# An adaptive-weight FFN in split fp32r on one core: moving the last pairs' gate, evictions and column steps

## The chip, the cores and the metric

The kernel runs on one core of a Trainium2 chip. The time is device microseconds of one execution; the median of three runs of the kernel before is 414.88 us (414.72 to 414.88). Engines are named as in the profile: PE (TensorE, matrix products), DVE (VectorE), ACT (ScalarE), POOL (GpSimd), SP (SyncE, which only queues DMAs here).

## The reference

The input x has 64 batches of 64 rows and 1024 columns. Each batch picks one of 16 matrices of 64 x 64, and its 64 rows are mixed by it. The mixed rows go through a 1024 x 1024 layer, and a small low-rank branch is added for the one of four experts that wins a linear gate. The result is added to x.

```python
W = weights[condition]                      # one 64 x 64 matrix per batch
m = einsum('bct,bcd->bdt', x, W)            # mix the 64 rows of each batch
logits = m @ gate_w.T + expert_bias         # 4 experts
top1 = argmax(logits)
base = einsum('bth,oh->bto', m, W_up)       # 1024 -> 1024
z = einsum('nh,erh->ner', m, lora_A)        # 4 experts x rank 8
d = einsum('ner,ehr->neh', z, lora_B)       # SCALE is 1
out = x + base + d[top1]
```

## The kernel before

**Order of the algebra.** Mixing rows and multiplying by weights commute, so the kernel multiplies x first, by a matrix of 1060 columns: 4 columns of the gate, 32 of lora_A and 1024 of W_up. That product is called u. It then applies the row mix to u (the block diagonal matrix `bd` holds two batches' matrices), takes gate and low-rank values from the first 36 columns, and adds the low-rank branch.

**Tiles.** 128 rows (two batches) are one block; there are 32 blocks, worked on in 16 pairs (a, b). A column half has 530 columns (NB), and a product over half of the 1024 inner elements has four k steps. To keep fp32's accuracy every factor is split in a high and a low part, and three matmuls (high x high, low x high, high x low) make one step; each is cut in two PSUM banks of 264 and 266 columns. A k step is thus six matmuls.

**Pairs and products.** The first two pairs use eight half products each (`eight`). The others use a scheme with seven (`seven`), for which the activations and the weights are summed first (S1 to S4, T1 to T4). `order` in `seven` lists the products. The last pair has six in its list; the seventh (S4 by B22) is done after the list by `product_by_bank`, one bank after the other, so that the first bank can be read while the second is computed. `c` is the name of the accumulators of products (three of 1024 columns), `o` that of smaller ones (two of 512 columns).

**Column steps.** A block's output is made in column steps, for most blocks of 356, 352 and 352 columns (`COLS`), for the last but one block (a of the last pair) of 356, 174, 258 and 272 (`LAST`). One column step is `apply` (three matmuls with `bd`), `delta` (one matmul adding the low-rank branch) and `evict`; `finish` is all three. The first step is split, since the gate needs its first 36 columns: `apply`, then `gate` (six small DVE operations that pick the expert and mask the low-rank values, to z), then `turn` (a transpose of z on PE, its two parts copied by ACT and DVE to zt), then `delta` and `evict`.

**Evictions.** For all blocks but the last two, `evict` copies `o` by ACT to a y tile; three y tiles exist. After the last column step POOL queues a DMA that adds x to the tile in place, and SP queues the store when it has landed. The last pair's two y tiles are loaded ahead with x: b's are added by DVE and stored by ACT's queue, column step by column step; a's first 494 columns go by ACT and an accumulating DMA (480 of them are then stored, 14 go with the next store), the rest by DVE and SP's queue. So in the last pair the block ahead (pb, block 29) has to use the y tile of the block before it (pa, block 28).

**What sets the order.** All instructions are kept in program order on their engine (`InOrder`, line 35). The program order is written by hand: `at(s, k, fn, ...)` puts a step into product s after k step k, and k = -1 ahead of the product. In the last pair, up to the change, step 3 is S3 by T3, step 4 is A22 by T4 (accumulator "4", b's first half), and step 5 is S1 by T1. pb's first step is evicted at (3, 2), its others finish at (3, 3) and (4, 1). The gate of a is at (4, 2), its `turn` at (5, 1) and its `delta` at (5, 2). `first_of_b` at (5, -1) makes the first 36 columns of b's u; `gate_of_b` at (5, 1) takes the gate from them in the first bank of an accumulator of its own, `ts["w"]`. A `c` buffer, `z`, receives the transpose of b's z in its first bank and b's first column step in its second.

In the profile nearly all lines are line 43, that of the helper which keeps program order, so tile names are what tells instructions apart: `uh`/`ul` are u's parts, `ah`/`al` those of activations, `bd` the row mix, `lg` to `z` the gate, `o<-ident,z` the transpose.

Of the kernel before, what the change touches and what calls it, by code (L numbers as in the profile page):

```python
# [46 lines left out]
def kernel(  # L47
# [28 lines left out]
    tensor, vector, scalar, pool, sync = (  # L76
        InOrder(tc, e) for e in (nc.tensor, nc.vector, nc.scalar, nc.gpsimd, nc.sync)
    )
# [17 lines left out]
    raw, As, us, ys, wsel, zs, os_, ts = ({} for _ in range(8))  # L96

    def temp(name):
        return tp.tile([P, NB], F32, name=name, tag="t")
# [95 lines left out]
    def chain():  # L195
        return psum.tile([P, 1024], F32, name="c", tag="c", bufs=3)
# [38 lines left out]
    def body(c):  # L235
        return c[:, LEFT : LEFT + NB]
# [7 lines left out]
    def u_low(i, n, src):  # L244
        h, lo = us[i]
        vector.tensor_sub(lo[:, n], src, h[:, n].bitcast(F32))

    def u_split(i, n, src):
        scalar.copy(u_tiles(i)[0][:, n], src)
        u_low(i, n, src)  # L250

    def half(hf):
        return slice(NB * hf, NB * hf + NB)

    def u_of(i, hf, c):
        u_split(i, half(hf), body(c))
# [5 lines left out]
    def u_sum(i, hf, c, t):  # L262
        u_add(i, c, t)
        u_split(i, half(hf), ts["u", i])
# [33 lines left out]
    STORED = FIRST // 16 * 16  # L298

    def place():  # L300
        return psum.tile([P, 512], F32, name="o", tag="o", bufs=2)
# [10 lines left out]
    def apply(i, j, o=None):  # L312
        c0, n = cols(i, j)
        o = os_[i, j] = place() if o is None else o
        cond_u(o[:, :n], i, slice(c0, c0 + n))
# [33 lines left out]
    def delta(i, j):  # L349
        s, d = ycols(i, j)  # L350
        tensor.matmul(
            os_[i, j][:, s], zs[i], b3[:, d], start=False, stop=True, skip_group_check=True
        )
# [22 lines left out]
    def finish(i, j, o=None):  # L376
        apply(i, j, o)
        delta(i, j)
        evict(i, j)
# [60 lines left out]
    u = raw[0, 0][:, k]  # L440
# [181 lines left out]
    def seven(g):  # L622
        a, b = 2 * g, 2 * g + 1
        last = g == NG - 1
        h = [[] for _ in range(7)]
        pa, pb = a - 2, a - 1
        cp = cs[g - 1]

        def at(s, k, fn, *args):
            h[s].append((k, fn, *args))  # L630

        def first_of_b():

            s = ts["last"] = temp("usum")
            q, r = slice(0, G), slice(G, NB)
            vector.tensor_add(s[:, q], body(c["4"])[:, q], ts["t7"][:, q])
            u_split(b, q, s[:, q])
            vector.tensor_add(s[:, r], body(c["4"])[:, r], ts["t7"][:, r])

        def gate_of_b():  # L640
            ts["w"] = chain()
            o = ts["w"][:, :512]
            cond_u(o[:, :G], b, slice(0, G))
            gate(b, o)
            u_split(b, slice(G, NB), ts["last"][:, G:])

        if g == 2:
            at(0, 0, apply, pa, 0)
            at(0, 0, gate, pa)
            at(0, 0, lambda: u_of(pb, 0, cp["1"]))  # L650
            at(0, 3, turn, pa)
            at(1, 0, delta, pa, 0)
            at(1, 0, evict, pa, 0)
            at(1, 1, finish, pa, 1)
            at(1, 2, finish, pa, 2)
            for k in range(KH):
                at(1 + k, 3, split_b, "T4", k)
            at(1, 3, apply, pb, 0)
            at(1, 3, gate, pb)
            at(2, 3, turn, pb)  # L660
        else:
            at(0, -1, lambda: u_sum(pb, 0, cp["2"], ts["t1"]))
            at(0, 1, finish, pa, 1)
            at(0, 3, finish, pa, 2)
            at(1, 2, apply, pb, 0)
            at(1, 2, gate, pb)
            at(2, 2, turn, pb)
        at(3, 2, delta, pb, 0)
        at(3, 2, evict, pb, 0)
        at(3, 3, finish, pb, 1)  # L670
        at(4, 1, finish, pb, 2)
        at(1, -1, lambda: keep("t1", c["1"]))
        if not last:
            order = (
                ("1", "A11", "B11", True),
                ("2", "S2", "T2", True),
                ("3", "S1", "T1", True),
                ("1", "A12", "B21", False),
                ("2", "S3", "T3", False),
                ("3", "S4", "B22", False),  # L680
                ("2", "A22", "T4", False),
            )
            at(0, 2, split_a, g, "S1")
            at(1, 0, split_a, g, "A12")
            at(2, 0, lambda: keep_sum("t6", c["2"], "t1"))
            at(2, 1, split_a, g, "S3")
            at(2, 2, split_cond, a)
            at(3, -1, lambda: keep_sum("t5", c["3"], "t1"))
            at(3, 2, split_a, g, "S4")
            at(4, -1, lambda: u_of(a, 0, c["1"]))  # L690
            at(4, 2, split_a, g, "A22")
            at(5, -1, lambda: u_add(b, c["2"], ts["t5"]))
            at(5, 0, apply, a, 0)
            at(5, 0, gate, a)
            at(5, 0, lambda: u_split(b, half(1), ts["u", b]))
            at(6, 0, turn, a)
            at(6, 0, lambda: u_sum(a, 1, c["3"], ts["t6"]))
            at(6, 2, delta, a, 0)
            at(6, 2, evict, a, 0)
            at(6, 3, split_cond, b)  # L700

            for i in (b + 2, a + 2):
                at(0, 0, load_half, i, 0)
                at(1, 0, load_half, i, 1)
            at(1, 3, load_cond, a + 2)
            at(3, 1, load_cond, b + 2)
            at(2, 3, sums, g + 1, "S1")
            at(3, 3, sums, g + 1, "S2")
            at(4, 3, sums, g + 1, "S3")
            at(5, 2, split_a, g + 1, "A11")  # L710
            at(6, 1, split_a, g + 1, "S2")
            at(6, 3, sums, g + 1, "S4")
            if g == NG - 2:
                for i in (a + 2, b + 2):
                    at(6, 0, load_y, i)
        else:

            order = (
                ("1", "A11", "B11", True),
                ("2", "S2", "T2", True),  # L720
                ("1", "A12", "B21", False),
                ("2", "S3", "T3", False),
                ("4", "A22", "T4", True),
                ("3", "S1", "T1", True),
            )
            at(0, 2, split_a, g, "A12")
            at(1, 0, split_a, g, "S3")
            at(2, 0, lambda: keep_sum("t6", c["2"], "t1"))
            at(2, 1, split_a, g, "A22")
            at(2, 2, split_cond, a)  # L730
            at(3, -1, lambda: u_of(a, 0, c["1"]))
            at(3, 0, split_a, g, "S1")
            at(3, 1, split_cond, b)
            at(4, -1, lambda: keep_sum("t7", c["2"], "t1"))
            at(4, 0, split_a, g, "S4")
            at(4, 2, apply, a, 0)
            at(4, 2, gate, a)
            at(5, -1, first_of_b)
            at(5, 1, turn, a)
            at(5, 1, gate_of_b)  # L740
            at(5, 2, delta, a, 0)
            at(5, 2, evict, a, 0)
            at(5, 3, lambda: finish(a, 1, ts["w"][:, 512:]))
        run(g, order, h, c)
        cs[g] = dict(c)
        if last:

            z = chain()
            turn(b, z[:, :512])
            u_add(b, c["3"], ts["t7"])  # L750
            scalar.copy(us[b][0][:, half(1)], ts["u", b])
            keep_sum("t8", c["3"], "t6")
            s = temp("usum")
            places = place(), place()

            def u_bank(m):
                n = LAST_BANKS[m]
                vector.tensor_add(s[:, n], places[m][:, : n.stop - n.start], ts["t8"][:, n])
                scalar.copy(us[a][0][:, NB + n.start : NB + n.stop], s[:, n])

            def u_bank_low(m):
                n = LAST_BANKS[m]
                u_low(a, slice(NB + n.start, NB + n.stop), s[:, n])

            product_by_bank(
                g,
                places,
                "S4",
                "B22",
                [(3, u_bank, 0), (3, lambda: u_low(b, half(1), ts["u", b]))],  # L770
            )
            u_bank(1)
            u_bank_low(0)
            finish(b, 0, z[:, 512:])
            u_bank_low(1)
            finish(b, 1, chain()[:, :512])
            sync.dma_start(out[a, :, :STORED], ys[a][:, :STORED])
            finish(b, 2, chain()[:, :512])
            finish(a, 2)
            finish(a, 3)  # L780
# [50 lines left out]
```

## Time and profile before

| What | us |
|---|---|
| median of three runs | 414.88 |
| the profiled execution | 415.4 |
| its span, first to last instruction | 413.6 |
| PE busy in the span | 408.5 |
| DVE, ACT, POOL busy | 285.6, 185.0, 75.0 |
| step 3 of the last pair starts on PE | 391.61 |
| last matmul starts / takes | 409.39 / 0.29 |

The table's first two rows are the time of an execution, the others are inside the span. A row of the timeline gives start, duration, engine, operation, tiles (out<-in), shape, and in brackets how long the engine sat idle before it and what ended that. Rows of the same shape that follow each other are merged (x2). Matmuls are pipelined: their durations overlap, so what one costs is the distance of two starts, 0.12 us for 264 columns. A row of the table by stretches gives the stretch, its length, busy time and number of instructions for PE, PEld (weight loads), DVE, ACT and POOL, then the granted clock of PE, the mean busy share of the 16 DMA engines and GB/s.

### The profile page before, as it was taken

How to read it: one execution, taken by the hardware profiler on the slowest of the kernel's cores; microseconds unless marked ns; L12 is line 12 of the kernel's file. 1: busy time of each engine (PE TensorE's matmuls, PEld its weight loads, DVE VectorE, ACT ScalarE, POOL GpSimd, SP SyncE). 2: the span in 40 equal slices, each digit the busy share in tenths (PEclk: the TensorE clock that was granted, in tenths of full speed). 3: DMA queues.
4: the chain of work that ended last, by engine and by line, in shares of the span. 5: the costliest groups of instructions: out<-in, count | busy, mean ns of one | idle time of the engine just before them, and what ended most of it. 6: DMA issues, size and time to landing. Idle time of an engine off the chain costs nothing.

```text
span 413.6 us, 8160 instructions
## 1 busy us (share of the span) xinstructions
PE 408.5 (99%) x3191; PEld 407.7 (99%) x3191; DVE 285.6 (69%) x648; ACT 185.0 (45%) x419; POOL 75.0 (18%) x92
## 2 busy tenths in 40 slices
PE   8999999999999999999999999999999999999996
PEld 8999999999999999999999999999999999999995
DVE  5987776876767666676676767666676676766766
ACT  5846734453534445333343534445333344533531
POOL 4304502020020202102020020202102020020000
PEclk9999999999999999999999999999999999999999
DMA  8889964553556435465453555434465443564345
GB/s 276 301 305 224 241 167 98 137 123 99 172 133 177 92 93 143 124 178 135 103 127 98 164 135 159 128 81 138 122 179 135 104 126 94 169 165 124 52 101 178
DMA packets 25830, 60.99 MB, mean 147 GB/s; under 512 B 3328, under 2 KB 5344, under 8 KB 25792
## 3 DMA queue, kind: packets, MB, share of 16 engines
q1 hardware_dynamic: 18112, 40.48, 27.2%
q0 software_dynamic: 6704, 19.21, 27.1%
q10 hardware_dynamic: 976, 0.79, 0.6%
q8 instruction: 25, 0.41, 0.4%
q14 instruction: 13, 0.11, 0.1%
HBM read 43.68 MB, written 16.78 MB: 146 GB/s over the span
## 4 chain that ended last, share of the span: by engine, by line
PE 97%; DMA 1%; issue 0%; POOL 0%; DVE 0%; POOLq 0%
PE c L43 81%; PE o L43 16%; DMA cond_sb<-in_cond_dram 1%; DVE y L43 0%; POOL which L43 0%; POOL condf L43 0%; POOLq L43 0%; POOLq L818 0%
## 5 line engine op out<-in xcount | busy, mean ns | idle before, releaser
L43 PE MATMUL c<-hT,ah 128*128 128x264 f32 x480 | 139.7, 291 | 0.0
L43 PE MATMUL c<-lT,ah 128*128 128x264 f32 x480 | 137.3, 286 | 0.0
L43 PE MATMUL c<-hT,al 128*128 128x264 f32 x480 | 137.1, 286 | 0.0
L43 PE MATMUL c<-hB,ah 128*128 128x264 f32 (+1 forms) x424 | 121.8, 289 | 0.0
L43 PE MATMUL c<-hB,al 128*128 128x264 f32 (+1 forms) x424 | 121.0, 287 | 0.0
L43 PE MATMUL c<-lB,ah 128*128 128x264 f32 (+1 forms) x424 | 119.0, 287 | 0.0
L43 PEld LDWEIGHTS c<-lT,ah 128*128 128x128 f32 x480 | 91.0, 190 | 0.0
L43 PEld LDWEIGHTS c<-hT,ah 128*128 128x128 f32 x480 | 90.9, 189 | 0.0
L43 PEld LDWEIGHTS c<-hT,al 128*128 128x128 f32 x480 | 90.6, 189 | 0.0
L43 POOL DMA_DIRECT2D y<-in_x_dram x31 | 29.3, 945 | 290.3 <-ACT y L43 285.3
L43 PEld LDWEIGHTS c<-hB,ah 128*128 128x128 f32 x424 | 80.7, 190 | 0.3 <-ACT hB L43 0.2
L43 PEld LDWEIGHTS c<-hB,al 128*128 128x128 f32 x424 | 80.7, 190 | 0.0
L43 PEld LDWEIGHTS c<-lB,ah 128*128 128x128 f32 x424 | 79.5, 190 | 0.2 <-issue 0.2
L43 ACT COPY y<-o 128x352 f32<-128x352 f32 (+1 forms) x91 | 40.1, 443 | 58.4 <-PE o L43 55.0
L43 ACT CAST uh<-usum 128x530 fp32r<-128x530 f32 (+4 forms) x44 | 27.1, 616 | 68.4 <-DVE usum L43 68.4
L43 DVE TENSOR_TENSOR al<-S,ah 128x512 fp32r<-128x512 f32 x56 | 38.5, 688 | 24.2 <-ACT ah L43 24.2
L43 DVE TENSOR_TENSOR al<-xh,ah 128x512 fp32r<-128x512 f32 x46 | 31.7, 689 | 30.0 <-ACT ah L43 30.0
L43 PE MATMUL o<-uh,bd 128*128 128x356 f32 (+2 forms) x186 | 44.7, 322 | 0.0
L43 DVE TENSOR_TENSOR ul<-usum,uh 128x530 fp32r<-128x530 f32 (+4 forms) x44 | 30.0, 682 | 18.6 <-ACT uh L43 18.6
L43 ACT CAST zt<-o 96x128 fp32r<-96x128 f32 x31 | 8.1, 262 | 76.0 <-PE o L43 76.0
L43 POOL DMA_INDIRECT wsel<-in_cw_dram,idx x32 | 34.9, 1089 | 10.6 <-issue 5.2
L43 ACT CAST ah<-S 128x512 fp32r<-128x512 f32 x56 | 34.9, 623 | 1.8 <-DVE S L43 1.4
(88 smaller groups left out, 471.3 us busy)
## 6 DMA issues: line engine op xcount, KB each, us to landing
xh<-in_xt_dram SPq DMA_DIRECT2D x60, 256.0 KB
y<-in_x_dram POOLq DMA_DIRECT2D x30, 512.0 KB, 5.6
out_dram<-y SPq DMA_DIRECT2D x30, 512.0 KB
wraw<-in_w_dram SPq DMA_DIRECT2D x23, 265.0 KB
T<-in_w_dram POOLq DMA_DIRECT2D x8, 265.0 KB, 7.3
xx<-in_xt_dram SPq DMA_DIRECT2D x1, 512.0 KB
wsel<-in_cw_dram,idx POOLq DMA_INDIRECT x32, 5.0
y<-in_x_dram SPq DMA_DIRECT2D x1, 512.0 KB
```

The lines of the kernel that those rows point to most:

```text
L43: return lambda *a, **k: self.tc.keep_in_program_order(fn(*a, **k))
```

## The change

Only what the last pair issues is changed. The block ahead's first step is evicted after k step 0 of step 3, and its others finish after (3, 1) and (4, 0). The gate of a moves to the end of step 3, its transpose to (4, 1), its `delta` and eviction to (5, 0), and its second column step to (5, 2), where it takes an `o` buffer in place of the second half of `ts["w"]`. The store of a's first 480 columns is queued in step 5, ahead of the last pair's other stores in SP's order. In the last product b's first column step is put between the two banks, and the low part of a's first bank after k step 1 of the second bank; the second bank's low part moves behind b's second column step.

```diff
-        at(3, 2, delta, pb, 0)
-        at(3, 2, evict, pb, 0)
-        at(3, 3, finish, pb, 1)
-        at(4, 1, finish, pb, 2)
+        for step, where in enumerate(((3, 0), (3, 1), (4, 0)) if last else ((3, 2), (3, 3), (4, 1))):
+            if step:
+                at(*where, finish, pb, step)
+            else:
+                at(*where, delta, pb, 0)
+                at(*where, evict, pb, 0)
...
-            at(4, 2, apply, a, 0)
-            at(4, 2, gate, a)
+            at(3, 3, apply, a, 0)
+            at(3, 3, gate, a)
+            at(4, 1, turn, a)
             at(5, -1, first_of_b)
-            at(5, 1, turn, a)
+            at(5, 0, delta, a, 0)
+            at(5, 0, evict, a, 0)
             at(5, 1, gate_of_b)
-            at(5, 2, delta, a, 0)
-            at(5, 2, evict, a, 0)
-            at(5, 3, lambda: finish(a, 1, ts["w"][:, 512:]))
+            at(5, 2, finish, a, 1)
+            at(5, 3, lambda: sync.dma_start(out[a, :, :STORED], ys[a][:, :STORED]))
...
-                [(3, u_bank, 0), (3, lambda: u_low(b, half(1), ts["u", b]))],
+                [
+                    (3, u_bank, 0),
+                    (3, lambda: u_low(b, half(1), ts["u", b])),
+                    (3, lambda: finish(b, 0, z[:, 512:])),
+                    (5, u_bank_low, 0),
+                ],
             )
             u_bank(1)
-            u_bank_low(0)
-            finish(b, 0, z[:, 512:])
+            finish(b, 1, chain()[:, :512])
             u_bank_low(1)
-            finish(b, 1, chain()[:, :512])
-            sync.dma_start(out[a, :, :STORED], ys[a][:, :STORED])
             finish(b, 2, chain()[:, :512])
             finish(a, 2)
             finish(a, 3)
```

## The prediction

> **What bounds the kernel now.** I read the page first: who is busy, and what chain ended last.
>
> ```profile
> PE 408.5 (99%) x3191; PEld 407.7 (99%) x3191; DVE 285.6 (69%) x648; ACT 185.0 (45%) x419; POOL 75.0 (18%) x92
> ...
> PE 97%; DMA 1%; issue 0%; POOL 0%; DVE 0%; POOLq 0%
> ```
>
> TensorE is busy 408.5 of 413.6 us. The change adds and removes no matmul and touches only what is issued after about 391.6 us. So there are two places where time can move: holes that appear in TensorE's row (today there are none there), and what follows its last matmul.
>
> Next the timeline of the last 20 us. First ScalarE (ACT) from step 3 of the last pair on, where the pair ahead is evicted:
>
> ```profile
> 391.86 0.60 ACT L43 CAST uh<-c 128x530 fp32r<-128x530 f32 x1
> 392.49 0.62 ACT L43 CAST ah<-S 128x512 fp32r<-128x512 f32 x1
> 393.02 0.51 ACT L43 CAST bd<-wsel 64x64 fp32r<-64x64 f32 x2
> 395.44 0.78 ACT L43 COPY y<-o 128x320 f32<-128x320 f32 x2 [1.91 <-DMA out_dram<-y]
> 396.24 0.62 ACT L43 CAST ah<-S 128x512 fp32r<-128x512 f32 x1
> ```
>
> The last row but one is the one to see. The eviction of pb's first columns (128x320) was computed by TensorE at 393.81+0.31 = 394.12, but ACT sat 1.91 us until 395.44: the y buffer that it writes still held the row block before, whose store (queued by SyncE at 392.71) had not landed. Nothing upstream of that store is moved by the change, so 395.44 stays. Today all urgent ACT work (uh, ah, bd) is ahead of this copy in ACT's queue, and nobody needs pb's buffer soon, so the wait is free.
>
> Then what the gate of a costs, and TensorE at the end:
>
> ```profile
> 398.92 0.16 DVE L43 TENSOR_TENSOR lg<-o,bias_sb 128x4 f32<-128x4 f32 x1 [1.33 <-PE o L43]
> ...
> 400.04 0.25 DVE L43 COPY z<-zm 128x96 f32<-128x96 f32 x1
> ...
> 400.94 0.27 PE L43 MATMUL o<-ident,z 128*96 128x128 f32 x1
> ...
> 409.39 0.29 PE L43 MATMUL o<-b,zt 96*128 96x272 f32 x1
> ```
>
> The gate takes 400.29-398.92 = 1.37 us on VectorE (DVE). The last matmul ends at 409.68, the last eviction at 410.16 (409.24+0.92), and the span at 413.6. What fills the 3.4 us after it, by stretches (the last two columns are DMA share and GB/s):
>
> ```profile
> 408.50:409.00 0.50, 0.50 (x6) 0.50 (x5) 0.50 (x2) 0.00 (x0) 0.00 (x0) 1.00 0.00 0
> 409.00:409.50 0.50, 0.50 (x6) 0.46 (x4) 0.50 (x2) 0.00 (x0) 0.00 (x0) 1.00 0.94 342
> ...
> 411.75:412.00 0.25, 0.00 (x0) 0.00 (x0) 0.00 (x0) 0.00 (x0) 0.00 (x0) 1.00 0.81 287
> 412.00:412.50 0.50, 0.00 (x0) 0.00 (x0) 0.00 (x0) 0.00 (x0) 0.00 (x0) 1.00 0.02 4
> ```
>
> Six stores are still to be moved at 409.0 (160, 240, 2 x 176 and 2 x 136 KB, 1.05 MB) and keep all 16 DMA engines full until about 412.05: 345 GB/s. The last store waits behind the others.
>
> **The change part by part.**
>
> *The tail (gain).* finish(b, 0) moves ahead of the second bank. Its four matmuls (0.49+0.33+0.31 as pitch: 0.64 us) only change places with the bank, so TensorE's end is unmoved; VectorE's y copy of 320 columns now comes right after ul of 530 columns, and its store leaves about 0.7 us earlier on its own clock. The 240 KB store of a leaves earlier too: its accumulating DMA was issued at 404.33 and the store at 408.30, 3.97 later; finish(a, 1) now ends one k step (0.73) sooner. So 400 KB leave the burst ahead of the rest. VectorE keeps up: y 320, ul 258, usum 272, y 352, ul 272 at pitches of 0.35 to 0.43 put ul 272 ready 0.25 us before its matmul (409.27); today it is 0.8 ahead. If that cover went, the cost would be that difference alone. What is left then is bounded by the last three stores, b's third (issued at about 409.4) and a's two (409.7, 410.19). The row gives 0.87 us from issue to data (first ACT issue 408.14, data from 409.0), so they start at 410.35, and 448 KB at 345 GB/s take 1.33: 411.7 instead of 412.05. Against this row stands the price of the Trainium skill ("DMA: Bandwidth & Descriptors", section on the anatomy of one DMA, SWDGE path; these stores are of the other kind): the variable part is bytes over 436 GB/s, which would give 1.05 us and 411.4, a gain of 0.65, but then the last store's own 410.19+0.87+0.4 = 411.47 is the limit, 0.58. I take the measured rate: **-0.38**, ends -0.2 and -0.58.
>
> *The pair ahead by two k steps.* delta and evict of pb go from (3, 2) to (3, 0), its two finishes from (3, 3) and (4, 1) to (3, 1) and (4, 0). TensorE's inputs are there: zt of pb is done at 391.66, and delta now comes at 392.34. But the copy of pb's first columns now stands in ACT's queue directly behind uh, ahead of ah (S1) and the two bd casts, and still starts at 395.44. The Trainium skill ("TensorE: Matmul & The Clock Gate", engine queue depths) says that the ACT and DVE queues are strictly first in, first out. This is the rule that speaks against the change, and the row of 1.91 us idle agrees as far as it can: nothing overtook. With it, everything behind the copy is held from 392.5 to 395.44. Were it not so, only the owner of the buffer would be late.
>
> *The gate of a, up a product (from (4, 2) to (3, 3), the transpose from (5, 1) to (4, 1)).* Two accumulators of 512 columns ("o") exist. In the new order pb's first columns hold one, and the second is free when the transpose of pb is read. finish(pb, 1) takes that one without a wait; the gate column of a has to take the one of pb's first columns, so its first matmul waits for ACT. Step 3 starts at 391.61, a k step takes 0.735, delta 0.15, a finish of 352 columns 0.65. The gate column is due at 391.61+0.735+0.15+0.735+0.65+1.47 = 395.35. The buffer is free at 395.44+0.43 = 395.87; with 0.13 for the wait and the weight load (390.65 to 390.77 at the transpose) it starts at 396.0. **Stall one: 0.65.**
>
> Second, z. ACT by the pitches of the rows: y 320 at 395.44, ah 395.76, y 352 at 396.28 (+0.53), bd 396.63 (+0.34), bd done 397.14. DVE's queue, in order: al of S1 from 396.41, bd from 397.01 to 397.5, and only then the gate: lg at 397.51, z done at 398.88, transpose at 399.06 (0.05 for the semaphore, 0.13 load). TensorE, already 0.65 late, comes there at 396.0+0.49+0.735+0.65+0.735 = 398.61, and waits again: **stall two: 0.45**, together **1.10** (399.06 against 397.96 with no stall). If the queues let work pass, only the 0.65 would remain: 415.4-0.38+0.65. Behind the waiting transpose stand k steps 2 and 3 of the product and everything after; the reader of zt, delta(a, 0), is at (5, 0) two k steps later (1.5 us) and zt needs about 1.2, so it is covered, as are S1's halves (needed at 400.6, ready at 397.1).
>
> *Others at nothing.* The first column sum of b (first_of_b) no longer stands behind a's gate on DVE, the gate of b comes with its z ready 0.4 us before the transpose at the end of step 5: that cover was 0.29 before. A store wait on SyncE holds no one: behind it are only later stores. finish(a, 1) uses an "o" buffer that is free since zt was read. The granted clock is 1.00 in all rows of the tail; I give two stalls of half a microsecond no price there.
>
> **Sum:** +1.10-0.38 = +0.72. The profiled execution took 415.4 with a span of 413.6: 416.1 in its terms. The median of runs without the profiler is 0.52 lower (414.88), and shifts alike: **415.6**, +0.17%. A kernel like this can be told from no change by about 0.2%, 0.83 us: 414.05 and 415.71 are the bounds.
>
> **The rivals.**
>
> A, as above: 415.6, own range 415.2 to 416.0. For it: each wait is in today's order already, only with slack that the change spends. Chance 53%, of which 17 lie beyond 415.71.
>
> B, a longer stall. The chain from the store's landing to the transpose is serial, so each 0.1 us of a later landing is 0.1 us of time. The accumulating DMA ahead of that store took 392.71-387.16 = 5.55 us here, and over the run 5.3 to 9.8 with a median of 5.6. At 0.1 later than profiled it decides for slower by over 0.2%; at 0.5 later the time is 416.1. Against: the last pair has no activation loads any more. Chance 30%.
>
> C, the other side: not slower, because the store lands early. Each 0.1 us of an earlier landing shortens both stalls; at 0.7 us before the profiled one (394.7) stall and gain cancel, and from 1.1 us before (394.3) only the tail counts: 414.88-0.38 = 414.5, or 414.3 at the outer bound. For it: in runs without the profiler the DMAs may be quicker. Against: 1.91 us idle in the row, and 5.3 as the quickest of the accumulating DMAs, a quarter of a microsecond below this one's. Chance 12%, of which 4 for faster than 414.05, which would need more than my outer bound.
>
> D, nothing happens: the stall is a third as long, and the shorter drain pays for it. 414.9. Chance 5%.
>
> Faster 4%, same 36+8+5 = 49%, slower 17+30 = 47%. The range leaves out most of C's lower half and B's far end: 414.5 to 416.4.
>
> **What will show it.** In the new profile: ACT's copy of 128x320 at 395.4 with a wait of about 2.9 us on the store (392.5 to 395.4) and ah of S1 after it; a hole of about 0.6 us on TensorE before the 356-column matmuls at about 396.0, and one of 0.4 before o<-ident,z at about 399.1; the last matmul ending at 410.8. In the tail: stores flowing from before 409.5 relative to the old clock, and 3.0 us from the last eviction to the end instead of 3.4. The prediction is wrong if TensorE has no hole before 399 us (then C), or if a third hole opens behind the transpose or at the last bank.

## The result

The median of 19 runs is 415.95 us (415.17 to 416.39), against 414.78 us for the kernel before in 19 runs beside it. The ratio is 1.0024, with a 95% interval of 1.0018 to 1.0030: the change costs 0.75 to 1.25 us. Forecast were 415.6 us, the range 414.5 to 416.4, and nearly even chances for "same" and "slower".

The profiled execution took 416.28 us with a span of 414.5 (before: 415.4 and 413.6). The page of the kernel after, the same rows as shown of before:

```profile
PE 408.6 (99%) x3191; PEld 407.5 (98%) x3191; DVE 285.7 (69%) x648; ACT 185.1 (45%) x419; POOL 75.5 (18%) x92
...
PE 91%; DMA 4%; DVE 2%; issue 2%; ACT 0%; DVEq 0%; POOLq 0%; ACTq 0%; SPq 0%
PE c L43 76%; PE o L43 15%; DMA y<-in_x_dram 3%; DMA out_dram<-y 1%; DVE y L43 1%; DVE ul L43 0%; DVE usum L43 0%; ACT y L43 0%; ACT ah L43 0%; DVE t L43 0%; DVE bd L43 0%; DVE zt L43 0%; ACT zt L43 0%; DVE z L43 0%; DVE zm L43 0%
```

PE's busy time is the same to 0.1 us, but the chain that ended last now runs back through 4% of DMA, above all the accumulating DMA into a y tile and a store from it. Where that enters is in the waits of the last 27 us of the kernel after (who <- for whom, us in total, times, longest):

```profile
PEld o L43 <- ACT y L43: 1.3, 2, 0.8
...
PE o L43 <- ACT y L43: 0.6, 1, 0.6
...
PE o L43 <- DVE z L43: 0.4, 1, 0.4
```

TensorE, which waited for nothing there before, now waits for an ACT copy to y and for z. Weight loads and matmuls sit side by side in this table, so its rows overlap and are not to be added. The timeline of ACT, DVE and PE after shows the order:

```profile
391.40 0.60 ACT L43 CAST uh<-c 128x530 fp32r<-128x530 f32 x1
395.13 0.43 ACT L43 COPY y<-o 128x320 f32<-128x320 f32 x1 [3.12 <-PE c L43]
395.58 0.62 ACT L43 CAST ah<-S 128x512 fp32r<-128x512 f32 x1
396.10 0.45 ACT L43 COPY y<-o 128x352 f32<-128x352 f32 x1
396.45 0.51 ACT L43 CAST bd<-wsel 64x64 fp32r<-64x64 f32 x2
...
396.23 0.69 DVE L43 TENSOR_TENSOR al<-S,ah 128x512 fp32r<-128x512 f32 x1 [3.48 <-ACT ah L43]
396.84 0.46 DVE L43 TENSOR_TENSOR bd<-wsel,bd 64x64 fp32r<-64x64 f32 x2
397.34 0.16 DVE L43 TENSOR_TENSOR lg<-o,bias_sb 128x4 f32<-128x4 f32 x1
...
398.46 0.25 DVE L43 COPY z<-zm 128x96 f32<-128x96 f32 x1
...
395.61 0.59 PE L43 MATMUL o<-uh,bd 128*128 128x356 f32 x2 [0.56 <-ACT y L43]
...
398.86 0.28 PE L43 MATMUL o<-ident,z 128*96 128x128 f32 x1 [0.37 <-DVE z L43]
...
410.18 0.29 PE L43 MATMUL o<-b,zt 96*128 96x272 f32 x1
```

ACT is idle for 3.12 us before the copy of pb's first columns; ah and bd come after it. DVE waits 3.48 us for ah, makes al and its own part of bd, and only then starts lg. PE has its two holes, 0.56 us before the gate column and 0.37 before the transpose. One label misleads: the 3.12 us are put down to "PE c". PE had been done with pb's columns since 391.88+0.31 = 392.19; in e2, e6, e7, e9 and e10 below, where ACT has the same order, the same wait carries the name of the store.

### The profile page after: what moved, and what is told of

It is laid out like the page before. It is cut to its first block, busy times and chain, and to the rows that moved or that the text cites. A ratio compares the mean times of both kernels' runs of the same rounds, so it can differ in the third digit from the quotient of the medians.

```text
span 414.5 us, 8160 instructions
## 1 busy us (share of the span) xinstructions
PE 408.6 (99%) x3191; PEld 407.5 (98%) x3191; DVE 285.7 (69%) x648; ACT 185.1 (45%) x419; POOL 75.5 (18%) x92
## 4 chain that ended last, share of the span: by engine, by line
PE 91%; DMA 4%; DVE 2%; issue 2%; ACT 0%; DVEq 0%; POOLq 0%; ACTq 0%; SPq 0%
PE c L43 76%; PE o L43 15%; DMA y<-in_x_dram 3%; DMA out_dram<-y 1%; DVE y L43 1%; DVE ul L43 0%; DVE usum L43 0%; ACT y L43 0%; ACT ah L43 0%; DVE t L43 0%; DVE bd L43 0%; DVE zt L43 0%; ACT zt L43 0%; DVE z L43 0%; DVE zm L43 0%
## 5 line engine op out<-in xcount | busy, mean ns | idle before, releaser
L43 PE MATMUL o<-uh,bd 128*128 128x352 f32 (+3 forms) x188 | 45.2, 321 | 0.6 <-ACT y L43 0.6
```

The source lines that it names most:

```text
L43: return lambda *a, **k: self.tc.keep_in_program_order(fn(*a, **k))
```

## The experiments

The profiles of different executions start up to a microsecond apart, so I take all times from one instruction that comes ahead of everything the change moves: the start of ACT's cast uh<-c of 128x530 in step 3. **D** is the start of pb's 128x320 copy after it (before: 395.44-391.86 = 3.58), and **lateness** is the end of the last matmul after it less that of the kernel before (409.68-391.86 = 17.82). **Tail** is the span's end less the last matmul's end (before: 413.59-409.68 = 3.91).

| Kernel | median us | ratio to before, 95% | D | lateness | tail |
|---|---|---|---|---|---|
| before | 414.78 | | 3.58 | 0 | 3.91 |
| the change | 415.95 | 1.0024 [1.0018, 1.0030] | 3.73 | 1.25 | 4.03 |
| e10 the change again | 415.65 | 1.0017 [1.0011, 1.0024] | 3.58 | 1.11 | 3.91 |
| e1 tail only | 414.62 | 0.9998 [0.9989, 1.0006] | 3.30 | -0.02 | 3.79 |
| e2 no tail | 415.81 | 1.0023 [1.0014, 1.0033] | 3.03 | 0.55 | 4.03 |
| e3 own y tiles | 414.39 | 0.9988 [0.9981, 0.9995] | 0.82 | -0.10 | 3.57 |
| e4 urgent first | 414.89 | 1.0000 [0.9991, 1.0008] | 3.26 | 0.30 | 3.94 |
| e5 gate only | 415.87 | 1.0025 [1.0017, 1.0034] | 3.31 | 1.03 | 4.07 |
| e6 pair only | 414.67 | 0.9994 [0.9985, 1.0002] | 3.58 | 0.05 | 3.82 |
| e7 block 28 sooner | 415.20 | 1.0007 [0.9999, 1.0016] | 2.93 | 0.47 | 4.22 |
| e8 own y tiles, before | 414.57 | 0.9994 [0.9986, 1.0002] | 2.29 | -0.01 | 3.69 |
| e9 zeros in the hole | 415.40 | 1.0009 [1.0001, 1.0017] | 3.28 | 0.82 | 3.66 |

Medians and ratios are of all runs of a kernel, the profiled execution among them; the last three columns are of that one execution. It can lie well away from its kernel's median (e10: 416.51 against 415.65; e8: 414.10 against 414.57), so a tenth of a microsecond in a column need not show in the median. e1 to e4, e5 to e8, and e9 with e10 ran on one chip each, with the kernel before beside them.

### Which part loses: e1, e2

e1 is the kernel before with only the last product changed:

```diff
-                [(3, u_bank, 0), (3, lambda: u_low(b, half(1), ts["u", b]))],
+                [
+                    (3, u_bank, 0),
+                    (3, lambda: u_low(b, half(1), ts["u", b])),
+                    (3, lambda: finish(b, 0, z[:, 512:])),
+                    (5, u_bank_low, 0),
+                ],
```

> Only the last product is changed: b's first column step between the two banks, the rest as before. Theory (the tail gains, the moved gate loses): no hole on TensorE, b's first store about 0.6 us sooner, the burst of stores 0.2 to 0.4 us shorter, time 414.4 to 414.7 against 414.8 before. Rival (the tail brings nothing, since the last two stores are bound by the last eviction and not by the burst): 414.8, with the end of the span 3.9 us after the last matmul as before. Rival (VectorE becomes the bound in the tail): 415.0 or more, with a's last eviction later relative to the last matmul.

It has no hole and can't be told from the kernel before: 0.9998, so at most 0.5 us of gain. b's first store leaves 0.67 us sooner before the last matmul's end, as expected, but the tail is only 0.12 us shorter in its profile, less than the 0.2 to 0.4 expected. VectorE keeps up.

e2 is the change with the last product of before:

```diff
-                    (3, lambda: finish(b, 0, z[:, 512:])),
-                    (5, u_bank_low, 0),
...
+            u_bank_low(0)
+            finish(b, 0, z[:, 512:])
```

> The change without its last part: pair ahead and gate moved, the last product as before. Theory (all of the loss is the gate that waits for the y tile's store through ACT's queue): the same two holes as in the change, about 0.6 and 0.4 us by their idle times, TensorE 1.1 to 1.25 us late; 415.9 to 416.0 without the tail's gain, 0 to 0.4 above the change. Rival (the new tail is what loses): at 415.0 or less.

1.0023, and 415.81 where 415.9 to 416.0 were expected: the whole loss is there without the new tail. Its lateness is only 0.55 in the profile, where 1.1 to 1.25 were expected, and the reason is in its ACT rows:

```profile
391.41 0.60 ACT L43 CAST uh<-c 128x530 fp32r<-128x530 f32 x1
394.44 0.43 ACT L43 COPY y<-o 128x320 f32<-128x320 f32 x1 [2.43 <-DMA out_dram<-y]
```

The store of block 28 landed 0.7 us sooner than in the first profile of the change (D 3.03 against 3.73), though the same work is queued ahead of it in the same order. Where the 0.7 us arise can be read from the steps before. From the moment when SyncE queues that store to the start of the copy it takes 2.71 to 2.73 us in all ten profiles in which block 29 uses the y tile: the store itself doesn't vary. The accumulating DMA ahead of it took 5.61 us in the change and 5.32 in e2, and it was queued 4.60 us ahead of the cast in the change and 5.00 in e2. That last difference is inherited, as block 28's own first copy had waited for a still older store, 0.4 us longer in the change (first row) than in e2 (second row):

```profile
382.17 0.43 ACT L43 COPY y<-o 128x320 f32<-128x320 f32 x1 [1.47 <-DMA out_dram<-y]
...
381.78 0.43 ACT L43 COPY y<-o 128x320 f32<-128x320 f32 x1 [1.07 <-DMA out_dram<-y]
```

### Is it the store: e3, e7, e8, e10

e3 is the change, with block 29 evicted to two temporary tiles of their own, in `evict`:

```diff
+        if i == NP - 3:
+            if j == 0:
+                ys[i] = [temp("y29") for _ in range(2)]
+            for t, lo, hi in zip(ys[i], (0, NB), (NB, H)):
+                p, q = max(d.start, lo), min(d.stop, hi)
+                if p < q:
+                    scalar.copy(t[:, p - lo : q - lo], o[:, p - d.start : q - d.start])
+                if j == 2:
+                    pool.dma_start(t[:, : hi - lo], x[i][:, lo:hi], accum_op=ALU.add)
+                    nc.sync.dma_start(out[i][:, lo:hi], t[:, : hi - lo])
+            return
```

> The change, with the pair ahead (block 29) evicted to two temporary tiles of 530 and 494 columns in place of the y tile whose store is still on its way, so one copy, one accumulating DMA and one store are in two pieces. Theory (landing of that store, then ACT's order): ACT's copy of 128x320 no longer waits, starts right behind uh about 0.7 us after step 3's second k step began, both holes on TensorE are gone, and the time is 414.4 to 414.8. Rival (the holes come from the two o buffers or from VectorE's gate being late whatever ACT does): one hole of 0.4 us or more stays, time 415.2 to 416.0.

```profile
391.47 0.60 ACT L43 CAST uh<-c 128x530 fp32r<-128x530 f32 x1
392.29 0.43 ACT L43 COPY y<-o 128x320 f32<-128x320 f32 x1 [0.22 <-PE o L43]
...
394.95 0.48 PE L43 MATMUL o<-uh,bd 128*128 128x356 f32 x2
...
397.56 0.27 PE L43 MATMUL o<-ident,z 128*96 128x128 f32 x1
```

The copy waits only for its matmul, both holes are gone: no row of PE has a bracket, no weight load waits, and the two matmuls of the gate column take 0.48 us and not the 0.59 that they take after a stall. (The missing bracket alone would not show it. In e2 and e4 the gate column has none either, but the weight load ahead of it waited 0.6 and 0.3 us.) The kernel is faster than both: 414.39, ratio 0.9988. TensorE's work, its order and the two o buffers are those of the change. What made it lose is the y tile that was not free.

e7 leaves the tiles and moves the store instead:

```diff
-            at(0, 1, finish, pa, 1)
-            at(0, 3, finish, pa, 2)
+            at(0, 0 if last else 1, finish, pa, 1)
+            at(0, 2 if last else 3, finish, pa, 2)
```

> The change, with the last two column steps of the block before the pair ahead (block 28) one k step sooner, so that its accumulating DMA and its store are queued about 0.5 us sooner. Theory (a serial chain from that landing to the transpose): both holes shrink by as much as the landing comes sooner, about 0.5 us in all; time 415.3 to 415.6. Rival (the DMA queue is busy then and the store lands when it did): 415.9.

The lateness falls to 0.47 and the time to 415.20, 0.1 better than the lower end of what was expected. The accumulating DMA is queued 5.28 us ahead of the cast, against 4.60 in the change, 4.70 in e10 and 5.00 in e2, so part of the difference to the change is the edit and part the chance seen in e2. The expectation that both holes shrink was wrong: the idle time before the transpose is 0.36 to 0.38 us in all five profiles of this order (the change, e2, e7, e9, e10), and only the first hole follows the landing. z and TensorE's arrival at the transpose both move with it, so their distance stays. e10 is the change once more:

> The change itself, beside the kernel with the zeros on the same chip: 415.9, two holes, the end of the span 4.0 us after the last matmul with the fetch at 5.5 us before it. Theory of the serial chain: TensorE's lateness is 1.10 us plus what the store's landing is later than 3.82 us after the start of step 3. Rival (the holes have fixed lengths): 1.25 us late as in the first profile, whatever the landing.

Now the forecast of a serial chain can be put to five profiles, with one formula and no new number: lateness = 1.10 + (D - 3.58).

| | D | formula | measured |
|---|---|---|---|
| the change | 3.73 | 1.25 | 1.25 |
| e10 the change again | 3.58 | 1.10 | 1.11 |
| e9 zeros in the hole | 3.28 | 0.80 | 0.82 |
| e2 no tail | 3.03 | 0.55 | 0.55 |
| e7 block 28 sooner | 2.93 | 0.45 | 0.47 |

All within 0.02 us. The rival, two holes of fixed lengths, is out: the second is fixed, the first is not. e10's fetch of instructions, in the expectation put at 5.5 us before the last matmul's end, came at 4.4.

e8 gives the kernel before the tiles of e3:

> The kernel before, with block 29 in two temporary tiles as in the kernel that did so with the change. Theory (in the kernel before nobody needs what the copy's wait holds up): ACT's wait of 1.6 to 1.9 us is gone and the time is that of the kernel before, 414.6 to 415.0; the gain of the change with such tiles is then the new tail's and order's. Rival (the tiles alone bring the gain): 414.4.

No lateness, as in the kernel before, and 414.57 with an interval that holds no change. The copy now waits for its own matmul in the later place that it has in this order. Between the medians of e8 and e3, on different chips, lie 0.18 us, which the intervals don't separate, so how much of e3's gain is the change's order and tail and how much the free tile stays open.

### What stands between the store and TensorE: e4, e5, e6

e4 queues S1's split and b's bd ahead of the copy that waits:

```diff
-            at(3, 0, split_a, g, "S1")
-            at(3, 1, split_cond, b)
+            at(3, -1, split_a, g, "S1")
+            at(3, -1, split_cond, b)
```

> The change, with S1's split and b's bd casts queued on ACT ahead of the copy that waits (at the start of step 3). Theory (two stalls: the o buffer of the pair ahead, and the gate behind ah, bd in the queues): the first hole stays (idle about 0.6 us before the 356 columns), the second, before the transpose, is gone or under 0.1 us; time 0.4 to 0.55 below the change, 415.4 to 415.5. Rival (what is behind in ACT's queue doesn't matter, z is late by the gate's own length): same as the change, 415.9. Rival (everything comes from the queue): both holes gone, 414.7.

```profile
PEld o L43 <- ACT y L43: 0.3, 1, 0.3
...
394.74 0.59 PE L43 MATMUL o<-uh,bd 128*128 128x356 f32 x2
...
397.49 0.28 PE L43 MATMUL o<-ident,z 128*96 128x128 f32 x1
```

The second hole is gone (nothing waits at the transpose) and the first is 0.3 us of idle time, at the weight load of the gate column; the lateness of 0.30 is the 0.65 of the first stall less the 0.32 that the store landed sooner than before (D 3.26). So the second hole was what is queued behind the copy on ACT and, through ah and bd, on DVE. The time is 0.5 better than expected. Between e4 and e10, on different chips, the intervals allow 0.1 to 1.4 us; the 0.45 of the second hole lies in it, and I can't say more.

e5 moves the gate of a alone (with all that the change does in step 5), e6 the pair ahead alone. The first lines of each, e5's and then e6's:

```diff
+            at(3, 3, apply, a, 0)
+            at(3, 3, gate, a)
+            at(4, 1, turn, a)
...
+        for step, where in enumerate(((3, 0), (3, 1), (4, 0)) if last else ((3, 2), (3, 3), (4, 1))):
```

> The gate of a moved up as in the change, the pair ahead and the last product as before. Theory (two o buffers, both held by the pair ahead until ACT has copied them): the gate column still waits for the copy of pb's first columns, and the transpose now for the copy of pb's last columns, which TensorE ends only just before: holes of about 0.3 to 0.6 and 0.85 us, 1.2 to 1.5 us in all, time 416.0 to 416.3. Rival (the loss comes from the pair ahead's move alone): 414.8.

> The pair ahead moved up by two k steps as in the change, the gate of a and the last product as before. Theory (the wait on the store harms only what needs the gate early): ACT waits about 2.4 to 3 us at the copy, but S1's halves, b's bd and the gate are in time, TensorE has no hole, time 414.7 to 415.0. Rival (everything behind the waiting copy in ACT's queue is late for TensorE): 415.5 or more.

e5 loses as much as the change, 1.0025. Both figures are under what was expected, a lateness of 1.03 for 1.2 to 1.5 and 415.87 us for 416.0 to 416.3, but both holes are there, and the second now waits for a copy:

```profile
398.09 0.31 PE L43 MATMUL o<-ident,z 128*96 128x128 f32 x1 [0.54 <-ACT y L43]
```

The early gate needs an o buffer that pb's copies hold, whichever order pb has. e6 has the longest kind of wait on ACT and loses nothing:

```profile
394.89 0.43 ACT L43 COPY y<-o 128x320 f32<-128x320 f32 x1 [2.98 <-DMA out_dram<-y]
```

Lateness 0.05, ratio 0.9994. A wait of 2.98 us is free as long as nobody needs the o buffer, ah and bd behind it; the earlier gate makes it expensive.

### Where the tail's gain went: e9

In the change b's first store left 2.26 us before the last matmul's end (408.21 against 410.47) where it had left 1.54 before it (408.14 against 409.68). That part came. The tail got no shorter all the same, for a's first store went later. The stretches of the kernel after (the last two columns: DMA share, GB/s):

```profile
409.50:410.00 0.50, 0.50 (x6) 0.50 (x6) 0.50 (x2) 0.00 (x0) 0.00 (x0) 1.00 0.17 56
410.00:410.50 0.50, 0.47 (x4) 0.25 (x2) 0.50 (x2) 0.00 (x0) 0.00 (x0) 1.00 0.39 143
410.50:411.00 0.50, 0.00 (x0) 0.00 (x0) 0.45 (x2) 0.00 (x0) 0.00 (x0) 1.00 0.93 327
...
412.50:412.75 0.25, 0.00 (x0) 0.00 (x0) 0.00 (x0) 0.00 (x0) 0.00 (x0) 0.71 1.01 361
412.75:413.00 0.25, 0.00 (x0) 0.00 (x0) 0.00 (x0) 0.00 (x0) 0.00 (x0) 0.50 0.45 153
```

The DMA engines are 0.17 and 0.39 busy from 409.5 to 410.5 and then full to about 412.85: b's first store was early, a's (SyncE, 409.98) wasn't. It waits for the accumulating DMA into a's tile, which took 404.35 to 409.98, 5.6 us, against 404.33 to 408.30, 3.97 us, before. What shares the DMA engines with it, in the queues of the kernel after from 404.9 to 406.9:

```profile
q1 hardware_dynamic: 122, 0.44, 56.5%
q0 software_dynamic: 26, 0.05, 22.1%
q8 instruction: 1, 0.02, 5.7%
...
y<-in_x_dram POOLq DMA_DIRECT2D x1, 247.0 KB, 5.6
```

The q1 packets are block 29's store, q0 the accumulating DMA, and q8 a fetch of instructions, one packet of 16 KB on one of the 16 engines. By its records it runs from 5.5 to 3.7 us before the last matmul's end; the rest of that store was through by 4.2, and the share of one engine only by 2.1. In the kernel before the fetch had ended (5.4) when the store's data began to move (5.1). The Trainium skill ("Runtime: NRT & Kernel Launch", instruction fetch mechanics) says that an engine's instructions are refilled in 16 KB blocks and that this is mostly hidden; here the size agrees, and the hiding is the question. Which engine's instructions they are, no view shows. To test whether the fetch can be moved, e9 adds to the change 16 instructions that do nothing to the result, where TensorE waits anyway (8 weight loads, and 8 matmuls that add one column of zeros to c["2"]):

```diff
+            at(3, 3, add_zeros, 8)
             at(3, 3, apply, a, 0)
             at(3, 3, gate, a)
```

> The change, with eight matmuls of one column that add zero to step 3's product, issued on TensorE just before the gate column that waits (they fill part of the first hole and put 16 instructions ahead of what follows). In the change a fetch of instructions (16 KB on one DMA engine) runs from 5.5 to 3.7 us before the last matmul's end, at the same time as the store of block 29; in the kernel before it had run from 6.4 to 5.4, ahead of that store. Theory (the tail's gain is lost since the fetch holds up one engine's share of that store, then of a's accumulating DMA, so that a's first store goes with the last ones): the fetch comes about 1 us sooner, a's store is queued more than 1 us before the last matmul ends, the span ends 3.6 to 3.8 us after it in place of 4.0, time 0.2 to 0.4 below the change run beside it. Rival (the accumulating DMA is late for another reason): tail 4.0, same time as the change, or up to 0.1 more where the zeros aren't covered.

The queues of e9 in two stretches that follow each other, 402.9 to 404.1 and 404.7 to 406.3:

```profile
q8 instruction: 1, 0.02, 5.1%
...
y<-in_x_dram POOLq DMA_DIRECT2D x1, 247.0 KB, 4.4
...
q1 hardware_dynamic: 102, 0.35, 56.9%
q0 software_dynamic: 18, 0.04, 24.9%
```

The fetch is over 5.9 us before the last matmul's end, ahead of the store (its data from 5.6 on), the accumulating DMA takes 4.4 us, a's store is queued 1.64 us before the end, and the tail is 3.66, 0.25 shorter than that of e10 beside it, as the theory had it. The time is 0.25 below e10's (415.40 and 415.65), but those intervals overlap: the times only point to it.

The traces of the kernels that have the new last product say the same. All figures are us before the last matmul's end, but for the tail:

| | fetch | block 29's store through | a's store queued | tail |
|---|---|---|---|---|
| e7 | 4.4 to 3.5 | 1.9 | 0.27 | 4.22 |
| the change | 5.5 to 3.7 | 2.1 | 0.49 | 4.03 |
| e4 | 5.4 to 4.0 | 2.4 | 0.82 | 3.94 |
| e10 the change again | 4.4 to 3.4 | 2.6 | 1.03 | 3.91 |
| e1 | 6.5 to 5.5 | 3.5 | 1.15 | 3.79 |
| e9 | 6.9 to 5.9 | 4.1 | 1.64 | 3.66 |

(e3, left out, has that store in two pieces.) a's accumulating DMA is queued 6.12 or 6.13 us before the end in five of the six, and 5.34 in e1. Where the fetch is over before the store's data move, the store is through early; where it falls into the store, the store is late, then a's store, and the tail is longer. What put the fetch where it was is less clear. In two executions of the same kernel, the change and e10, it starts 5.5 and 4.4 us before the end, so of the move to 6.9 in e9 up to a microsecond can be chance.

## Why the prediction came out as it did

*No hole today, all work of TensorE kept:* right. 408.5 and 408.6 us busy, and the lateness of e1, e6 and e8 is 0.05 us at most.

*Stall one, 0.65, and stall two, 0.45, from ACT's copy at 395.44:* right in place and cause, and in size to 0.27 us. Predicted were starts 396.0 and 399.06 on the clock of the kernel before; measured are 395.61 and 398.86 on one that is 0.46 us ahead (391.40 against 391.86), so 396.07 and 399.32. They are later by 0.07 and 0.26. The landing was 0.15 later; TensorE then started 0.48 us after the copy did, where 0.56 was put, which takes back half of that in the first. The rest of the second is a pitch that the prediction had too short: ah follows the copy's start by 0.45 us (395.13 to 395.58), where it put 0.32, and all of ACT and DVE behind it, lg too, is late by that. Against e3, which has the same order without a stall, the transpose comes 1.22 us late in e10 and 1.37 in the change, where 1.10 was predicted. That the lateness to the kernel before is 1.11 in e10, where D is that of before, is in part luck: the stall was 0.12 more, and the new order without stalls ends 0.10 sooner (e3), which the prediction didn't have.

*ACT and DVE first in, first out:* e4 shows it. The two sums given were 1.10 with it and 0.65 without; the order on ACT alone decided between them.

*That 395.44 stays, since nothing upstream of the store moves:* true of the order, but not of one execution. D runs from 3.03 to 3.73 over kernels that issue the same work up to there, for the reasons given at e2. Rival B's price (0.1 us of time for each 0.1 of landing) is right to 0.02 us; that its store comes earlier as easily as later was not in it. C's wording, that an earlier landing shortens both stalls, holds for their sum alone, for the second stayed at 0.36 to 0.38 us of idle time.

*The tail, -0.38:* this is the term that failed; without it the forecast would have been 415.98, for a median of 415.95. Measured is +0.12 in the profile of the change and 0 in e10. The step behind it was that a's store leaves earlier since finish(a, 1) ends one k step sooner. Its accumulating DMA was issued 6.1 instead of 5.35 us before the last matmul's end, as said, but it landed no sooner, as block 29's store, held up by a fetch of instructions, stood in its way; fetches I had not looked for. Where the fetch lies elsewhere the gain is 0.25 (e9), and e3 has 0.34, so the -0.38 was also somewhat large. The span's 0.9 us between the two profiles are thus made of 1.25 (lateness) + 0.12 (tail) - 0.46 (the earlier start).

*The step from 416.1 to 415.6:* the prediction took the 0.52 us between one profiled execution and the median of three runs for a shift that each kernel has. It is no constant: the profiled execution lies 0.33 above its kernel's median in the change, 0.86 above in e10 and 0.47 below in e8. That it came to about the right size is luck, and the medians of the change itself, 415.95 and 415.65 in its two series, are nearly as far apart as the forecast and the first of them.

*The rivals.* C's point, an early landing, was on the right axis, but no landing reached the 0.7 us that it needed: the earliest one in a kernel that keeps block 28 in place is 0.55 sooner than before. D's, that stall and drain cancel, is out.

## What to carry to other kernels

A wait on one engine that costs nothing is a debt of the order around it: before moving a consumer up, look at which buffer it will take, who has to empty it, and what that engine is waiting for, since everything queued behind comes late with it. Here the cure was a free tile for one copy, which turned a loss of 1 us into a gain of 0.5. When a step moves, ask of its DMAs what shares their engines at the new time, and count the instruction fetches among them.

## What the runs showed that was not expected

The store of a block lands at times that differ by 0.7 us between executions with the same work ahead of it (D from 3.03 to 3.73), and none of it arises in the store, which takes 2.71 to 2.73 us from its queueing to the copy that waited for it. The accumulating DMA ahead of it varies by 0.36 us (5.25 to 5.61), and the rest is lateness handed on through the y tiles from an older store. And one fetch of 16 KB on one DMA engine, which is 5% of the DMA engines' time in a stretch of 1.2 us, fell together with a 512 KB store of which at least 15 parts in 16 were through in time and the rest came 1.2 to 2.4 us later (e2, e4, e5, e7, the change, e10), and with it everything that waits for the whole of the transfer. In the one execution profiled, sixteen tiny instructions some 8 us ahead of it had it out of the way.
